# Two attention layers on one core: output projections of layer 0 grouped, two pairs' scores in a row at some block ends, normalisation in two parts

## The chip, the cores and the metric

The kernel runs on one core of one Trainium2 chip. A core has a matrix engine (TensorE, PE in the profile, with PEld for its weight loads), three engines for other arithmetic (VectorE or DVE, ScalarE or ACT, GpSimd or POOL), and a queue, SP, from which most transfers are issued. The metric is device time in microseconds (us). All data is 32-bit floating point.

## The reference

The input x has 4 batches of 128 channels and 64 x 64 = 4096 positions ("tokens"). Two layers follow one another.

Layer 0 is attention over all positions with a head of 64 channels, an output projection and a residual:

```
q, k, v = wq x, wk x, wv x            # 64 x 4096 each
att = softmax(k^T q)                  # 4096 x 4096
x   = x + wo (att applied to v)       # 128 x 4096
```

Layer 1 is causal attention over layer-normalised tokens with a head of 128, and then a recurrent FFN:

```
t = t + softmax(causal(LN(t) Wq (LN(t) Wk)^T / sqrt(128))) LN(t) Wv
h = LN(t) W, normalised over all 4 x 4096 tokens
y_t = sigmoid(h_t + V y_(t-1))        # along the tokens
t = t + y
```

## The kernel before, in words

The kernel has a fast path and a general path that is only entered where a check on the device fails; all that follows is the fast path.

**Tiles and loops.** The 4096 rows of an attention are done in 8 blocks of 512 (g = 0 to 7), the keys in tiles of 128. One step of the main loop deals with a pair of key tiles. In layer 0 every block has 16 pairs; in layer 1, which is causal, block g has 2g + 2. The order is: batch 0 layer 0 (128 pairs), batch 0 layer 1 (72 pairs), batch 1 layer 0, and so on. For a pair,

- `scores` makes a 128 x 1024 tile of scores in PSUM (s_ps, two buffers) and ScalarE takes the exponential into p (four buffers, tag "p" of pool "prob");
- `values`, two pairs later (SKEW = 2), multiplies p with the values and adds to the accumulator acc in PSUM, of which there is one buffer. Layer 0 works with the array split in tiles of 64 x 64 for scores and values, layer 1 and all projections with the full 128 x 128;
- `sums` adds p to dsum on VectorE, for the softmax's denominators. A p buffer is free when values and sums have both read it.

**The end of a block.** With the last pair's values, `values` empties the accumulator: in layer 0 ScalarE copies it to "half" (128 x 1024) and VectorE adds the two halves into agg. VectorE also adds the two halves of dsum into den. A chain of later steps is then started, `finish0` or `finish1`, a Python generator: each `yield n, step` asks for the step n pairs later. One due step at most is run per pair; where none is due, one of the list `side` is run, which holds the next batch's queries, keys and values.

In layer 0 the chain is: `folded` (sums of den over partitions, through a transpose on VectorE and DMAs to and from DRAM); then `project`, which is not run when due but put on a list `fill`, from which one entry is taken at the end of the next block of layer 0, or of a block g > 0 of layer 1; then `normed`, one pair later; then `by_channels`, two pairs after that, which turns the normalised tokens around through DRAM into xhT. So block g is projected at the end of block g + 1, and block 7 at the end of layer 1's block 1. `project` makes reciprocals of the denominators, four products of 128 columns into o_ps (one buffer of the two that all small PSUM uses share), and four operations on VectorE that join the result to the residual in xs. `normed` makes the layer norm on VectorE: statistics and their aggregation for four groups of tokens, the variance, a power of -1/2 on GpSimd (ln_rstd, line 458), one Newton step of four small operations on VectorE (lines 459 to 462), and four operations that write xh.

In layer 1 `finish1` does the same work with `wv1` for its projection, stores xs to x2, normalises, transposes, and multiplies with the FFN's weights (wx_ps). VectorE takes statistics of that product and ScalarE copies it into xs.

`rows1`, called at the end of the block two before, makes the rows of layer 1's block from xhT (r_ps). So layer 1's block 6 asks for xhT's block 6 at the end of its block 4.

**The order of the work.** The Python order of these calls is not the order on the engines: the framework reorders instructions within an engine, and `keep_in_program_order` pins an instruction to its place. [...] On TensorE the order around the change is: scores, values, scores, values, and at a block's end projection or rows, if any.

The lines named later: L806 and L815 scores of layers 0 and 1, L820 and L822 their exponentials, L866 and L874 values, L846 sums, L885 half, L605 products of the projection, L610 joins, L570 rows, L745 and L755 statistics and copy of the FFN product, L458 to L462 power and Newton step.

Of the kernel before, what the change touches and what calls it, by code (L numbers as in the profile page):

```python
# [9 lines left out]
F32 = mybir.dt.float32  # L10
AF = mybir.ActivationFunctionType
ALU = mybir.AluOpType
# [3 lines left out]
P = 128  # L16
BLK = 512
# [332 lines left out]
def fast_path(  # L350
# [105 lines left out]
    def rsqrt(y, var, z):  # L456

        nc.gpsimd.tensor_tensor(y, var, mhalf[:, : y.shape[-1]], ALU.pow)  # L458
        nc.vector.tensor_tensor(z, y, y, ALU.mult)  # L459
        nc.vector.tensor_tensor(z, z, var, ALU.mult)  # L460
        nc.vector.tensor_scalar(z, z, -0.5, 1.5, ALU.mult, ALU.add)
        nc.vector.tensor_tensor(y, y, z, ALU.mult)  # L462

    with tc.tile_pool(name="batch", bufs=1) as batch, tc.tile_pool(name="rows", bufs=2) as rowp, tc.tile_pool(
# [7 lines left out]
        def misc(name):  # L472
            return ps_m.tile([P, BLK], F32, tag="m", name=name)
# [23 lines left out]
        bs = [Batch() for _ in range(B)]  # L497
        for bt in bs:
            bt.next = []


        def cols0(b, m):
# [91 lines left out]
                nc.sync.dma_start(out=own, in_=by_token.rearrange("q r k j -> (q r) k j"))  # L594
            return own

        def project(layer, b, g, agg, own):

            rec = recs[:, layer, b, ts(g, TPB)]

            tc.keep_in_program_order(nc.vector.tensor_reduce(rec, own.rearrange("p q j -> p j q"), AX.X, ALU.add))
            nc.vector.reciprocal(rec, rec)
            op = misc("o_ps")
            for j in range(TPB):
                nc.tensor.matmul(  # L605
                    op[:, ts(j, P)], lhsT=agg[:, ts(j, P)], rhs=wv1 if layer else wo2, start=True, stop=True
                )
            for j in range(TPB):
                t = xs[:, b, ds(g * BLK + j * P, P)]
                nc.vector.scalar_tensor_tensor(  # L610
                    t, in0=op[:, ts(j, P)], scalar=rec[:, j : j + 1], in1=t, op0=ALU.mult, op1=ALU.add
                )

        def normed(b, g, dst):

            st = stat.tile([P, TPB, nc.vector.BN_STATS_DIM], F32, tag="st", name="ln_st")
            mv = stat.tile([P, TPB, nc.vector.BN_AGGR_DIM], F32, tag="mv", name="ln_mv")
            for j in range(TPB):
                nc.vector.bn_stats(st[:, j], xs[:, b, ds(g * BLK + j * P, P)])  # L619
                nc.vector.bn_aggr(mv[:, j], st[:, j])  # L620
            var = stat.tile([P, TPB], F32, tag="var", name="ln_var")
            nc.vector.tensor_scalar(var, mv[:, :, 1], LN_EPS, None, ALU.add)  # L622
            y = stat.tile([P, TPB], F32, tag="rstd", name="ln_rstd")
            rsqrt(y, var, stat.tile([P, TPB], F32, tag="z", name="ln_z"))
            for j in range(TPB):
                nc.vector.tensor_scalar(  # L626
                    dst[:, j], xs[:, b, ds(g * BLK + j * P, P)], mv[:, j, 0:1], y[:, j : j + 1], ALU.subtract, ALU.mult
                )
# [31 lines left out]
        def finish0(b, g):  # L660

            agg, den = bs[b].agg, bs[b].den

            def norm():
                if g == 0:
                    bs[b].xh = batch.tile([P, NT, P], F32, tag="xh", name="xh")
                    bs[b].xhT = batch.tile([P, N], F32, tag="xhT", name="xhT")
                normed(b, g, bs[b].xh[:, ts(g, TPB)])
# [13 lines left out]

            def rest():
                yield 1, norm
                yield 2, by_channels

            def first():
                own = folded(den, False)

                def second(s):  # L690
                    project(0, b, g, agg, own)
                    push(s, rest())

                fill.append(second)

            yield 1, first

        def finish1(b, g):
            agg, den = bs[b].agg, bs[b].den
# [9 lines left out]
            def first():  # L709
                if final:  # L710

                    nc.scalar.activation(spare, agg[:, 0:1], AF.Sigmoid)
                project(1, b, g, agg, mem["own"])
# [7 lines left out]
                normed(b, g, mem["xh"])  # L721

            def second():
                mem["xhT"] = wk.tile([P, BLK], F32, tag="xhT2", name="xhT2")
# [37 lines left out]
            def sums():  # L762
                mem["own"] = folded(den, by_pe)

            if by_pe:
                yield 1, lambda: (sums(), first())
            else:
                yield 1, sums
                yield 3, first
            yield 3, second  # L770
            yield 1 if final else 6 if g < 2 or g == NB - 1 else 4, third


# [82 lines left out]
        def values(it):  # L856

            bt = bs[it.b]
            if it.first:
                bt.acc = ps_a.tile([P, 2, BLK], F32, tag="a", name="acc")  # L860
            for h, (t, q0, n, o) in enumerate(it.at):
                if it.layer == 0:

                    for r in range(2):
                        part = slice(r * M, r * M + M)
                        nc.tensor.matmul(  # L866
                            bt.acc[h * M : h * M + M, r],
                            lhsT=bt.v[part, t % (NT // 2), t // (NT // 2)],
                            rhs=it.p[part, o : o + n],
                            start=it.first,  # L870
                            stop=it.last,
                        )
                else:
                    nc.tensor.matmul(  # L874
                        bt.acc[:, 0, q0:],
                        lhsT=bt.xh[:, t],
                        rhs=it.p[:, o : o + n],
                        start=it.first and h == 0,
                        stop=it.last and h == 1,
                    )  # L880
            if it.last:
                bt.agg = wk.tile([P, BLK], F32, tag="agg", name="agg")
                if it.layer == 0:
                    half = wk.tile([P, 2, BLK], F32, tag="half", name="half")
                    nc.scalar.copy(half, bt.acc)  # L885
                    nc.vector.tensor_tensor(bt.agg, half[:, 0], half[:, 1], ALU.add)
                else:
                    nc.scalar.copy(bt.agg, bt.acc[:, 0])
                bt.den = wk.tile([P, BLK], F32, tag="den", name="den")
                nc.vector.tensor_tensor(bt.den, it.den[:, 0], it.den[:, 1], ALU.add)  # L890

        waiting = []
        fill = []

        def push(slot, chain):
            step = next(chain, None)
            if step:
                waiting.append((slot + step[0], step[1], chain))
# [36 lines left out]
        started = []  # L935
        rows()
        rows()
        for s in range(len(items) + SKEW + 16):
            if s < len(items):
                it = items[s]  # L940
                if it.first:
                    bs[it.b].rows = bs[it.b].next.pop(0)
                    if it.layer and it.g == 3 and it.b + 1 < B:
                        for m in range(NB // 2):
                            side += keys(it.b + 1, m)
                scores(it)
            if 0 <= s - SKEW < len(items):
                it = items[s - SKEW]
                values(it)
                if it.last:  # L950
                    rows()
                    tokens()

                    if fill and (it.layer == 0 or it.g):
                        fill.pop(0)(s)
                    push(s, (finish1 if it.layer else finish0)(it.b, it.g))
            if s < len(items):
                sums(items[s])
# [12 lines left out]
        assert not waiting and not side and not fill  # L971

# [161 lines left out]
```

## Time and profile before

| | |
|---|---|
| median of 3 runs | 2074.14 us (2073.96 to 2077.06) |
| the profiled execution's own time | 2073.56 us |
| its span, first to last instruction | 2071.9 us |
| PE, PEld busy | 2052.6, 894.6 us |
| DVE, ACT, POOL busy | 1488.9, 993.6, 117.8 us |
| instructions of PE, DVE, ACT, POOL | 11716, 2865, 1071, 221 |
| clock granted to TensorE | 0.998 |

By stretches of the timeline, layer 0 of a batch takes some 237 us (242 in the first) and layer 1 some 257 us; the FFN's recurrence after the last block takes about 80 us.

How to read it: the page comes from one profiled execution. "busy" is the sum of an engine's instructions. Matmuls overlap and their ends are modelled, so two starts say more than one duration. In the timeline each row has start and duration in us, engine, source line, operation, output<-inputs, their shapes, and how many alike were merged; brackets hold the idle time before it and what ended that. A 32-bit product shows as two matmul instructions: 8 rows of s_ps or acc in layer 0 are the scores or values of one pair. "PE acc L866 <- ACT half L885" reads: that matmul waited for that copy.

### The profile page before, as it was taken

Reading aid. Unit: us, or ns where it says so; the run is one execution under the profiler, and the core shown is the slowest. Engines: PE = TensorE matmul, PEld = TensorE weight load, DVE = VectorE, ACT = ScalarE, POOL = GpSimd, SP = SyncE. Lnnn points to the kernel's source line nnn. Section 1 sums busy time; section 2 is a strip of 40 time slices with the busy share of each in tenths; the row PEclk is TensorE's granted clock in tenths of the full one; section 3 lists DMA queues with packets and bytes.
Section 4 is the critical chain, followed back from the end, with each engine's and each line's share of the span. In section 5 each row is a group of like instructions: output and inputs, shape, how many; then the busy total and the mean of one; then the engine's idle time right before and its main releaser. Section 6 shows DMA issues by size and latency. Waiting matters only on the chain.

```text
span 2071.9 us, 30792 instructions
## 1 busy us (share of the span) xinstructions
PE 2052.6 (99%) x11716; PEld 894.6 (43%) x11716; DVE 1488.9 (72%) x2865; ACT 993.6 (48%) x1071; POOL 117.8 (6%) x221
## 2 busy tenths in 40 slices
PE   9999999999999999999999999999999999999998
PEld 3333354444333344444333335444433334444456
DVE  4899975544889986554689997554578998655578
ACT  5666632333666643333466663323366665333365
POOL 1000010000000011000000001000000001100000
PEclk9999999999999999999999999999999999999999
DMA  3110123200110113311010012230001011201044
GB/s 113 53 20 15 22 57 76 68 16 16 57 22 13 22 32 72 78 37 24 16 53 16 19 22 57 68 75 16 16 17 17 17 22 27 51 21 26 16 168 164
DMA packets 207149, 89.03 MB, mean 43 GB/s; under 512 B 140961, under 2 KB 189601, under 8 KB 205969
## 3 DMA queue, kind: packets, MB, share of 16 engines
q1 hardware_dynamic: 205984, 86.42, 16.6%
q8 instruction: 94, 1.54, 0.3%
q14 instruction: 63, 0.51, 0.1%
q0 software_dynamic: 288, 0.39, 0.1%
q10 hardware_dynamic: 720, 0.16, 0.0%
HBM read 45.84 MB, written 36.89 MB: 40 GB/s over the span
## 4 chain that ended last, share of the span: by engine, by line
PE 82%; DVE 14%; issue 1%; ACT 1%; POOL 1%; DMA 0%; DVEq 0%; ACTq 0%; POOLq 0%
PE s_ps L815 22%; PE acc L874 22%; PE s_ps L806 14%; PE acc L866 14%; DVE dsum L846 9%; PE o_ps L605 2%; PE y_ps L1031 2%; PE r_ps L570 1%; PE wx_ps L742 1%; PE kr_ps L513 1%; ACT p L820 1%; PE v_ps L525 1%; DVE xr L1052 1%; POOL ln_rstd L458 1%; DVE xs L610 1%
## 5 line engine op out<-in xcount | busy, mean ns | idle before, releaser
L846 DVE TENSOR_TENSOR dsum<-dsum,p 128x1024 f32<-128x1024 f32 x676 | 825.2, 1221 | 394.9 <-ACT p L822 304.5
L820 ACT ACTIVATE p<-s_ps,nshift 128x1024 f32<-128x1024 f32 x512 | 571.2, 1116 | 324.3 <-PE s_ps L806 267.3
L822 ACT ACTIVATE p<-s_ps 128x1024 f32<-128x1024 f32 (+2 forms) x288 | 274.5, 953 | 605.1 <-PE s_ps L815 591.2
L866 PE MATMUL acc<-p,v 64*64 64x512 f32 x4096 | 532.2, 590 | 1.9 <-ACT half L885 1.9
L806 PE MATMUL s_ps<-swap,kr 64*64 64x512 f32 x2048 | 528.2, 592 | 2.0 <-ACT p L820 1.8
L806 PE MATMUL s_ps<-kr 64*64 64x512 f32 x2048 | 528.2, 592 | 0.3
L815 PE MATMUL s_ps<-rows,xhT 128*128 128x512 f32 (+3 forms) x1152 | 502.9, 559 | 0.0
L874 PE MATMUL acc<-p,xh 128*128 128x512 f32 (+3 forms) x1152 | 500.9, 557 | 0.0
L874 PEld LDWEIGHTS acc<-p,xh 128*128 128x128 f32 x1152 | 216.2, 190 | 244.3 <-issue 233.7
L815 PEld LDWEIGHTS s_ps<-rows,xhT 128*128 128x128 f32 x1152 | 214.1, 190 | 245.5 <-issue 209.3
L866 PEld LDWEIGHTS acc<-p,v 64*64 64x64 f32 x4096 | 155.1, 133 | 284.8 <-issue 270.4
L806 PEld LDWEIGHTS s_ps<-swap,kr 64*64 64x64 f32 x2048 | 138.4, 133 | 138.8 <-issue 123.7
L806 PEld LDWEIGHTS s_ps<-kr 64*64 64x64 f32 x2048 | 138.4, 133 | 138.0 <-issue 121.0
L458 POOL TENSOR_TENSOR ln_rstd<-ln_var,mhalf 128x4 f32<-128x4 f32 x64 | 68.8, 1075 | 1181.5 <-DVE ln_var L622 1181.5
L854 DVE TENSOR_TENSOR dsum<-dsum,p 128x256 f32<-128x256 f32 (+1 forms) x120 | 55.9, 498 | 53.4 <-POOL p L826 53.4
L610 DVE SCALAR_TENSOR_TENSOR xs<-o_ps,recs,xs 128x128 f32<-128x128 f32 x256 | 73.4, 343 | 3.7 <-PE o_ps L605 0.5
L626 DVE TENSOR_SCALAR xh<-xs,ln_mv,ln_rstd 128x128 f32<-128x128 f32 x256 | 71.4, 342 | 2.2
L826 POOL TENSOR_SCALAR_AFFINE_SELECT p<-p 128x128 f32<-128x128 f32 x128 | 38.2, 322 | 511.9 <-ACT p L822 506.2
L619 DVE BATCH_NORM_STATS2 ln_st<-xs 128x6 f32<-128x128 f32 x256 | 63.5, 269 | 0.0
L459 DVE TENSOR_TENSOR ln_z<-ln_rstd 128x4 f32<-128x4 f32 x64 | 10.4, 163 | 69.9 <-POOL ln_rstd L458 69.9
L755 ACT COPY xs<-wx_ps 128x512 f32<-128x512 f32 x31 | 18.1, 585 | 72.0 <-DVE stats L745 72.0
L844 DVE COPY dsum<-p 128x1024 f32<-128x1024 f32 x60 | 41.0, 684 | 11.7 <-ACT p L822 8.1
(138 smaller groups left out, 1023.4 us busy)
## 6 DMA issues: line engine op xcount, KB each, us to landing
xs<-in_xT SPq DMA_DIRECT2D x32, 256.0 KB, 3.0
by_r<-sqT SPq DMA_DIRECT2D x128, 64.0 KB, 2.2
xhT<-by_r SPq DMA_DIRECT2D x128, 64.0 KB, 2.0
x<-xs SPq DMA_DIRECT2D x32, 256.0 KB, 2.3
xr<-x SPq DMA_DIRECT2D x8, 1024.0 KB, 11.9
out_x<-xr SPq DMA_DIRECT2D x16, 512.0 KB, 3.5
by_c<-sqT SPq DMA_DIRECT2D x124, 64.0 KB, 1.8
xhT<-by_c SPq DMA_DIRECT2D x31, 256.0 KB, 2.7
```

The lines of the kernel that those rows point to most:

```text
L458: nc.gpsimd.tensor_tensor(y, var, mhalf[:, : y.shape[-1]], ALU.pow)
L610: nc.vector.scalar_tensor_tensor(t, in0=op[:, ts(j, P)], scalar=rec[:, j : j + 1], in1=t, op0=ALU.mult, op1=ALU.add)
L619: nc.vector.bn_stats(st[:, j], xs[:, b, ds(g * BLK + j * P, P)])
L626: nc.vector.tensor_scalar(dst[:, j], xs[:, b, ds(g * BLK + j * P, P)], mv[:, j, 0:1], y[:, j : j + 1], ALU.subtract, ALU.mult)
L806: nc.tensor.matmul(ps[c * M : c * M + M, off : off + n], lhsT=bs[it.b].kr[part, h, ds(t % (NT // 2) * P + c * M, M)], rhs=rows[h], start=True,
L815: nc.tensor.matmul(ps[:, off : off + n], lhsT=lhsT, rhs=rhs, start=True, stop=True)
L820: nc.scalar.activation(it.p[:, :off], ps[:, :off], AF.Exp, bias=nshift)
L822: nc.scalar.activation(it.p[:, :off], ps[:, :off], AF.Exp, scale=float(P) ** -0.5)
L846: nc.vector.tensor_tensor(flat, flat, it.p, ALU.add)
L854: nc.vector.tensor_tensor(den[:, h, q0:], den[:, h, q0:], it.p[:, o : o + n], ALU.add)
L866: nc.tensor.matmul(bt.acc[h * M : h * M + M, r], lhsT=bt.v[part, t % (NT // 2), t // (NT // 2)], rhs=it.p[part, o : o + n], start=it.first ...
L874: nc.tensor.matmul(bt.acc[:, 0, q0:], lhsT=bt.xh[:, t], rhs=it.p[:, o : o + n], start=it.first and h == 0, stop=it.last and h == 1,)
```

## The change

- Projections of layer 0 are made at set places, named in a table `visits`: blocks 0 and 1 at the end of block 2, blocks 2 and 3 at the end of block 4, block 4 at the end of 6, block 5 at the end of 7, and blocks 6 and 7 at the ends of layer 1's blocks 2 and 3. The list `fill` is gone. Until then the block's result waits in its own part of xhT, which is allocated at the end of block 0 and into which agg is now written.
- `project` is split into `denominators` (asked for 9 pairs after the fold), `projected` (the products, at the visit) and `joined` (one pair later, or nine for the second block of a visit).
- `normed` is split: `moments` has statistics, variance and the power on GpSimd and follows the join; the Newton step (`newton`) and the writing of xh come one pair later, with the Newton step's first instruction pinned to program order. In `finish1` likewise, but for the very last block, where both follow at once.
- At the ends of layer 0's blocks that have no visit (0, 1, 3 and 5) the scores of two pairs are made in a row, ahead of the next values; where the next pair's scores are due, they are already done.

```diff
+    def newton(y, var, z, pinned=False):
+        ins = nc.vector.tensor_tensor(z, y, y, ALU.mult)
+        if pinned:
+            tc.keep_in_program_order(ins)
...
-        def project(layer, b, g, agg, own):
+        def denominators(layer, b, g, own):
             rec = recs[:, layer, b, ts(g, TPB)]
             tc.keep_in_program_order(nc.vector.tensor_reduce(rec, own.rearrange("p q j -> p j q"), AX.X, ALU.add))
             nc.vector.reciprocal(rec, rec)
+
+        def projected(layer, agg):
             op = misc("o_ps")
...
+            return op
+
+        def joined(layer, b, g, op):
...
-        def normed(b, g, dst):
+        def moments(b, g):
...
-            rsqrt(y, var, stat.tile([P, TPB], F32, tag="z", name="ln_z"))
+            nc.gpsimd.tensor_tensor(y, var, mhalf, ALU.pow)
+            return mv, var, y
+
+        def normed(b, g, dst, mv, var, y, pinned=True):
+            newton(y, var, stat.tile([P, TPB], F32, tag="z", name="ln_z"), pinned)
...
             def first():
                 own = folded(den, False)
-                def second(s):
-                    project(0, b, g, agg, own)
-                    push(s, rest())
-                fill.append(second)
+                mem.append(own)
+
+            def leave(late):
+                op = projected(0, agg)
+                def rest():
+                    yield 1 + late, lambda: (joined(0, b, g, op), mem.append(moments(b, g)))
+                    yield 1, norm
+                    yield 2, by_channels
+                return rest()
+
+            bs[b].leave[g] = leave
             yield 1, first
+            yield 9, lambda: denominators(0, b, g, mem[0])
...
             if by_pe:
-                yield 1, lambda: (sums(), first())
+                yield 1, lambda: (sums(), first(), final and norm())
             else:
                 yield 1, sums
                 yield 3, first
-            yield 3, second
+            if not final:
+                yield 1, norm
+            yield 2, second
...
             if it.last:
-                bt.agg = wk.tile([P, BLK], F32, tag="agg", name="agg")
                 if it.layer == 0:
+                    if it.g == 0:
+                        bt.xhT = batch.tile([P, N], F32, tag="xhT", name="xhT")
+                    bt.agg = bt.xhT[:, ts(it.g, BLK)]
...
-        fill = []
+        visits = [{2: (0, 1), 4: (2, 3), 6: (4,), 7: (5,)}, {2: (6,), 3: (7,)}]
...
+        done = -1
+        def begin(s):
+            nonlocal done
+            if done < s < len(items):
+                done = s
...
+                scores(it)
+
+        for s in range(len(items) + SKEW + 16):
+            begin(s)
+            if SKEW < s < len(items) - 1 and items[s - SKEW].first and items[s + 1].layer == 0:
+                ended = items[s - SKEW - 1]
+                if ended.layer == 0 and ended.g not in visits[0]:
+                    begin(s + 1)
...
-                    if fill and (it.layer == 0 or it.g):
-                        fill.pop(0)(s)
+                    for k, g in enumerate(visits[it.layer].get(it.g, ())):
+                        push(s, bs[it.b].leave[g](8 * k))
                     push(s, (finish1 if it.layer else finish0)(it.b, it.g))
```

More of the change, by code (lines that the diff above doesn't have):

```diff
@@ L458, in rsqrt @@
         nc.gpsimd.tensor_tensor(y, var, mhalf[:, : y.shape[-1]], ALU.pow)
-        nc.vector.tensor_tensor(z, y, y, ALU.mult)
+        newton(y, var, z)
+    def newton(y, var, z, pinned=False):
+        ins = nc.vector.tensor_tensor(z, y, y, ALU.mult)
+        if pinned:
+            tc.keep_in_program_order(ins)
         nc.vector.tensor_tensor(z, z, var, ALU.mult)
@@ L499, in fast_path @@
             bt.next = []
+            bt.leave = {}
         def cols0(b, m):
@@ L607, in project @@
                 )
+            return op
+        def joined(layer, b, g, op):
+            rec = recs[:, layer, b, ts(g, TPB)]
             for j in range(TPB):
@@ L662, in finish0 @@
             agg, den = bs[b].agg, bs[b].den
+            mem = []
             def norm():
@@ L666, in norm @@
                     bs[b].xh = batch.tile([P, NT, P], F32, tag="xh", name="xh")
-                    bs[b].xhT = batch.tile([P, N], F32, tag="xhT", name="xhT")
-                normed(b, g, bs[b].xh[:, ts(g, TPB)])
+                normed(b, g, bs[b].xh[:, ts(g, TPB)], *mem.pop())
             def by_channels():
@@ L681, in by_channels @@
                     )
-            def rest():
-                yield 1, norm
-                yield 2, by_channels
             def first():
                 own = folded(den, False)
-                def second(s):
-                    project(0, b, g, agg, own)
-                    push(s, rest())
-                fill.append(second)
+                mem.append(own)
[7 more added lines that the diff above has]
+            bs[b].leave[g] = leave
             yield 1, first
+            yield 9, lambda: denominators(0, b, g, mem[0])
         def finish1(b, g):
@@ L712, in first @@
                     nc.scalar.activation(spare, agg[:, 0:1], AF.Sigmoid)
-                project(1, b, g, agg, mem["own"])
+                denominators(1, b, g, mem["own"])
+                joined(1, b, g, projected(1, agg))
                 if final:
@@ L720, in first, with norm @@
                 mem["xh"] = wk.tile([P, TPB, P], F32, tag="xh2", name="xh2")
-                normed(b, g, mem["xh"])
+                mem["of"] = moments(b, g)
+            def norm():
+                normed(b, g, mem["xh"], *mem["of"], not final)
             def second():
@@ L887, in values @@
                 else:
+                    bt.agg = wk.tile([P, BLK], F32, tag="agg", name="agg")
                     nc.scalar.copy(bt.agg, bt.acc[:, 0])
@@ L892, in fast_path @@
         waiting = []
-        fill = []
+        visits = [{2: (0, 1), 4: (2, 3), 6: (4,), 7: (5,)}, {2: (6,), 3: (7,)}]
+        assert NB == 8
         def push(slot, chain):
@@ L937, in fast_path @@
         rows()
-        for s in range(len(items) + SKEW + 16):
-            if s < len(items):
+        done = -1
[3 more added lines that the diff above has]
+                done = s
                 it = items[s]
@@ L944, in fast_path @@
                         for m in range(NB // 2):
-                            side += keys(it.b + 1, m)
+                            side.extend(keys(it.b + 1, m))
                 scores(it)
+        for s in range(len(items) + SKEW + 16):
[4 more added lines that the diff above has]
+                    begin(s + 1)
             if 0 <= s - SKEW < len(items):
@@ L970, in fast_path @@
                     form_half()
-        assert not waiting and not side and not fill
+        assert not waiting and not side
     with tc.tile_pool(name="xr", bufs=1) as xrp, tc.tile_pool(name="y", bufs=2) as yp, tc.tile_pool(
```

## The prediction

> **What bounds the kernel now.** I read the page's busy times first, then its chain that ended last, then the waits by engine, then the timeline of TensorE (PE) at single places. The first two:
>
> ```profile
> PE 2052.6 (99%) x11716; PEld 894.6 (43%) x11716; DVE 1488.9 (72%) x2865; ACT 993.6 (48%) x1071; POOL 117.8 (6%) x221
> PE 82%; DVE 14%; issue 1%; ACT 1%; POOL 1%; DMA 0%; DVEq 0%; ACTq 0%; POOLq 0%
> ```
>
> PE is busy 99% and carries 82% of the chain, so time can come only out of the matrix stream. "Busy" hides small losses, because the ends of matmuls are modelled; they show in distances between starts. This is PE around the end of block 0 of batch 0, layer 0 (columns: start, duration):
>
> ```profile
> 51.01 0.59 PE L806 MATMUL s_ps<-swap,kr 64*64 64x512 f32 x2
> ...
> 51.87 1.04 PE L866 MATMUL acc<-p,v 64*64 64x512 f32 x8
> 52.73 0.60 PE L806 MATMUL s_ps<-swap,kr 64*64 64x512 f32 x2
> ...
> 54.19 0.64 PE L866 MATMUL acc<-p,v 64*64 64x512 f32 x1 [0.42 <-ACT half L885]
> ```
>
> A step (scores or values of one pair) takes 0.86 us from start to start (51.01, 51.87, 52.73). The last distance is 1.46: the next block's values need the only accumulator, which the copy "half" on ScalarE (ACT) still empties. **Loss 0.60**; in the other three batches 546.44 to 547.96, loss 0.66. The step after it is 0.05 long (0.91), as after every stop below.
>
> At the ends of blocks 1 to 5 an output projection stands in that place:
>
> ```profile
> 79.99 1.04 PE L866 MATMUL acc<-p,v 64*64 64x512 f32 x8
> 80.96 1.16 PE L605 MATMUL o_ps<-wo,agg 128*128 128x128 f32 x8
> 82.05 0.65 PE L806 MATMUL s_ps<-swap,kr 64*64 64x512 f32 x2
> ...
> 82.96 0.61 PE L866 MATMUL acc<-p,v 64*64 64x512 f32 x4
> ```
>
> Its four 128-column products are worth one step, 0.86. Distances are 0.97, 1.09, 0.91: **0.39 lost** per visit in going from 64*64 tiles to 128*128 and back.
>
> Third, VectorE (DVE). Sums of a block's first pairs run late behind projection and normalisation, where DVE also waits for GpSimd's (POOL's) power:
>
> ```profile
> 87.17 0.17 DVE L622 TENSOR_SCALAR ln_var<-ln_mv 128x4 f32<-128x4 f32 x1
> 88.58 0.16 DVE L459 TENSOR_TENSOR ln_z<-ln_rstd 128x4 f32<-128x4 f32 x1 [1.24 <-POOL ln_rstd L458]
> ```
>
> I call lag the time from the end of a pair's exponential to the start of its sum. It peaks at 5.13 at the visit of 80 us, then 5.42, 5.70, 5.85, 5.86, 4.96. A sum frees one of four p buffers, so large lag holds ACT, and then PE:
>
> ```profile
> 179.53 1.04 PE L866 MATMUL acc<-p,v 64*64 64x512 f32 x8
> 180.60 0.65 PE L806 MATMUL s_ps<-kr 64*64 64x512 f32 x2
> ```
>
> 1.07 for 0.86. The losses are 0, 0, 0.07, 0.22, 0.23, 0 for those six lags: above about 5.65 PE loses what the lag exceeds. With 0.05 after each, **0.67 per batch**.
>
> Fourth, a place in batches 1 to 3 where layer 1's last FFN product meets the lag:
>
> ```profile
> 543.01 0.59 ACT L755 COPY xs<-wx_ps 128x512 f32<-128x512 f32 x1 [3.27 <-DVE stats L745]
> ```
>
> The statistics start at 542.29 behind eight back-to-back sums, the ACT copy waits for them, exponentials queue behind the copy, and PE goes from 543.03 to 544.67: **0.84 lost** with the 0.05.
>
> [...]
>
> **The change, part by part.** In the order of the changed program, layer 0 has eight o_ps products in a row at the ends of blocks 2 and 4, four beside r_ps at the end of 6 and four at the end of 7 as before; blocks 6 and 7 follow in layer 1 at the ends of its blocks 2 and 3. Ends 0, 1, 3, 5 have scores, scores, values, values. The products themselves are as many as before: nothing there.
>
> 1. Visits at 1, 3, 5 go: 3 x 4 batches x 0.39 = **-4.7**. Their "half" must now be hidden by the second scores, as at block 0. At 52.73 the second would start at 53.59 (its buffer is free: that exponential ended at 53.23) and end at 54.45, after 54.19, when values could run; in batch 1, 548.16 after 547.96. Cover is 0.26 and 0.20 to spare. Without it each end would lose 0.71.
> 2. Block 0's stop goes: 0.65 + 3 x 0.71 = **-2.8**.
> 3. Second products in 8 visits: between nothing (same mode) and 0.11 (r_ps at 225.21, o_ps at 226.18: 0.97 for 0.86). I take 0.05: **+0.4**. One more projection per batch in layer 1, where 256.91, 257.80, 259.57 give 0.03 and 0.06: 4 x 0.09 = **+0.4**.
> 4. Lag. Normalisation is split, so a sum stands between variance and newton; DVE's 1.24 wait becomes useful. But the order puts both blocks' joins and moments right behind the double visit; only the second newton comes seven sums later. From 83.22 of the trace: join and statistics as before to 85.85; three of the second block's joins (0.26 each) and two short ones, 86.9. The third pair's exponential now ends about 85.2 (visit 0.9 longer): lag 1.7. Then sum 1.14, the last join and second statistics 1.6, two sums 2.5, newton 0.81, xh 1.16, transpose 0.64: 94.7 against the sixth exponential's end at 90.4: **lag 4.4**. Seven sums recover 0.39 each (1.72 pitch less 1.33), the second newton part adds 2.6: 4.2. Three more sums and den, fold and transpose at the block's end (+1.6, as 0.43 became 2.05 at 107) give about 4.7, on a short copy. All below 5.65; by the end of the block without visit it is worked off (12 x 0.39). So 4 x 0.67 = **-2.7**.
> 5. At 527.15 the variance is ready; the sum that began at 528.37 can go before the wait, so the chain up to 531.88 is 0.9 earlier, and so are the eight sums and the copy of 543.01. PE lost 0.79 there, so it fits: 3 x 0.84 = **-2.5**.
> 6. Layer 1: pinned newtons on DVE, with sums, statistics and the by-channel DMAs on SP behind them. A layer 1 pair holds PE 3.43 us against DVE's 1.33, and PE has no wait there: nothing. Without that cover a POOL wait is 1.2 for each of 40. Blocks 6 and 7 come about 70 us later, but their rows are asked for only at the ends of blocks 4 and 5 of layer 1, 30 us or more after the visit; two DMA hops at 2.2 and 2.0 us fit. The order of SP's queue keeps the denominators' DMAs ahead of their use by several pairs. The tail after the last block keeps its order: nothing.
>
> Sum: -4.7 - 2.8 + 0.8 - 2.7 - 2.5 = -11.9. The profiled execution took 2073.56 (span 2071.9 and 1.7 around it), so 2061.7; the median 2074.14 is 0.6 above it: **2062.3**.
>
> **Rivals.**
> - *Only the matrix part comes* (0.13): DVE's lag and the stop at 543 stay, because a burst of two blocks replaces the waits saved. Speaks for it: lag stood at 5.4 with one block. Against: my 4.4. 2062.3 + 5.2 = 2067.5.
> - *The cover fails* (0.06): "half" is scheduled behind one more exponential (1.12), and the 16 plain ends each lose 0.71. Gains 1 and 2 turn into 12 x (0.71 - 0.39) = +3.8 and 0: 2062.3 + 7.5 + 3.8 = 2073.6. Against: the new ACT order has "half" before both exponentials.
> - *Nothing is gained otherwise* (0.03): [...] near 2072.
> - *Slower* (0.04): the double burst at the ends of 2 and 4 overruns the p buffers. It decides when the eight bursts cost PE over 11.9, that is 1.5 each, lag 7.15 or 2.7 above my sum; at lag 7.5, 8 x 1.9 = 15: about 2077.
> - The main case holds 0.74.
>
> **How the numbers follow.** A change of 0.2% is 4.1 us, about what a measurement of this kernel can tell from none. Main case and first rival are beyond it: faster 0.87; cover and nothing: 0.09; slower 0.04. The main case has its own range 2059.5 to 2065: all of layer 0's extra distance is 7.0 per batch, of which 3.3 goes, and a different order of layer 1's v_ps excursions (0.36 each, twelve) may give or take 1.5. With the first rival to 2069, no more than 2 in 10 is outside.
>
> **What would show it.** Steps 1 and 2: PE waits on "half" near nothing; values at plain ends 0.86 after the second scores. Step 3: o_ps to o_ps 0.86 to 0.97. Step 4: no wait on POOL in layer 0, lag peaks under 5.65 and no 1.07 distances. Step 5: the copy after the statistics near 542 minus what came before, with PE at 0.86. Layer 1 near 257 us per batch, as now. Wrong would be: "half" or p waits on PE, lag above 5.65, or longer layer 1.

## The result, and the profile after

| | before | changed kernel |
|---|---|---|
| median (range, runs) | 2075.43 us (2073.96 to 2077.06, 6) | 2066.5 us (2064.51 to 2067.79, 6) |
| ratio | | 0.9956, interval 0.9943 to 0.9969 |
| profiled execution, its span | 2073.56, 2071.9 us | 2065.22, 2063.5 us |
| first scores start at | 12.90 | 13.90 |
| from there to the end of the span | 2059.0 us | 2049.6 us |

The change makes the kernel 0.44% faster, 8.9 us by the medians. The forecast was 2062.3 with a range of 2059.5 to 2069.0, so the sign and the range held, and the likeliest case was 4.2 us too fast. The main case's own range ended at 2065; the result is inside the stated range only because that was stretched to 2069 for the first rival. The six times before fall into two groups, 2073.96 to 2074.14 and 2076.72 to 2077.06, with the median between them, so the 8.9 is known to a microsecond or two only.

The fifth row is the one to compare kernels by. The start of a profile varies: the first scores wait for the first transfers, and they began between 12.9 and 15.0 in the profiles of this study; two profiles of the changed kernel itself have 13.90 and 13.30. From the first scores on, the change is worth 2059.0 - 2049.6 = **9.4 us**, where the sum of the prediction had 11.9. Most of this section asks where those 2.5 us went.

First the page of the changed kernel, busy times and chain:

```profile
PE 2046.0 (99%) x11716; PEld 896.4 (43%) x11716; DVE 1492.2 (72%) x2865; ACT 990.1 (48%) x1071; POOL 135.5 (7%) x221
PE 97%; DVE 1%; issue 1%; DMA 0%; ACT 0%; POOL 0%; DVEq 0%; POOLq 0%; ACTq 0%
```

The counts are the same as before, so nothing was saved in work. VectorE has gone from 14% of the chain to 1%. One number has grown that the change was not meant to touch: GpSimd's busy time, from 117.8 to 135.5.

Second, TensorE around the end of block 0 of batch 0, the place shown at 51.87 before:

```profile
52.88 1.04 PE L895 MATMUL acc<-p,v 64*64 64x512 f32 x8
53.73 0.60 PE L835 MATMUL s_ps<-swap,kr 64*64 64x512 f32 x2
...
54.59 0.60 PE L835 MATMUL s_ps<-swap,kr 64*64 64x512 f32 x2
...
55.45 1.90 PE L895 MATMUL acc<-p,v 64*64 64x512 f32 x16
```

and ScalarE there:

```profile
54.13 1.01 ACT L917 COPY half<-acc 128x1024 f32<-128x1024 f32 x1
```

Starts are 52.88, 53.73, 54.59, 55.45: three steps of 0.86. The copy "half" ends at 55.14 and the accumulator is needed at 55.45. Before, where the values did wait, they began 0.05 behind the end of the copy (at 54.19, for 54.14), so of the 0.31 some 0.26 is to spare; in the first blocks of the other batches it is 0.20. The stop of 0.60 is gone, and no matmul of TensorE waits on "half" any more. (Its weight loads, which run ahead, still show 16 such waits of at most 0.5; they delay no matmul.)

Third, the first double visit, at the end of block 2:

```profile
107.81 1.04 PE L895 MATMUL acc<-p,v 64*64 64x512 f32 x8
108.78 2.05 PE L614 MATMUL o_ps<-wo,xhT 128*128 128x128 f32 x16
110.76 0.65 PE L835 MATMUL s_ps<-swap,kr 64*64 64x512 f32 x2
...
111.67 1.04 PE L895 MATMUL acc<-p,v 64*64 64x512 f32 x8
```

From 107.81 to 111.67 are 3.86 us for four steps' worth of work, one of values, two of projections, one of scores; four steps of 0.86 are 3.44, which leaves 0.42. A single visit lost 0.39 before. The second product of a visit costs 0.03 beyond its own step.

Fourth, VectorE behind that visit, at the first normalisation:

```profile
117.19 0.17 DVE L636 TENSOR_SCALAR ln_var<-ln_mv 128x4 f32<-128x4 f32 x1
117.27 2.55 DVE L875 TENSOR_TENSOR dsum<-dsum,p 128x1024 f32<-128x1024 f32 x2
119.73 0.16 DVE L462 TENSOR_TENSOR ln_z<-ln_rstd 128x4 f32<-128x4 f32 x1
```

Two sums stand between variance and Newton step, and there is no idle time. Of the 64 Newton steps, all of which waited for the power before, five still do. The lag (end of an exponential to start of its sum) peaks at 4.13 behind this visit and at 4.27 at the end of block 3, and is back at 0.03 before block 4 ends, where the next visit is. Both are under 5.65, and no step of 1.07 is left.

Fifth, the place where the forecast failed, layer 1's last FFN product in batch 1. The power and the start of the Newton step there before, on GpSimd and VectorE:

```profile
527.25 1.01 POOL L458 TENSOR_TENSOR ln_rstd<-ln_var,mhalf 128x4 f32<-128x4 f32 x1 [16.70 <-DVE ln_var L622]
```

```profile
528.29 0.16 DVE L459 TENSOR_TENSOR ln_z<-ln_rstd 128x4 f32<-128x4 f32 x1 [1.13 <-POOL ln_rstd L458]
```

VectorE in the changed kernel:

```profile
525.68 0.17 DVE L636 TENSOR_SCALAR ln_var<-ln_mv 128x4 f32<-128x4 f32 x1
525.76 1.22 DVE L875 TENSOR_TENSOR dsum<-dsum,p 128x1024 f32<-128x1024 f32 x1
527.88 0.16 DVE L462 TENSOR_TENSOR ln_z<-ln_rstd 128x4 f32<-128x4 f32 x1 [0.90 <-POOL ln_rstd L638]
...
530.46 10.49 DVE L875 TENSOR_TENSOR dsum<-dsum,p 128x1024 f32<-128x1024 f32 x8
540.87 0.69 DVE L772 BATCH_NORM_STATS2 stats<-wx_ps 128x6 f32<-128x512 f32 x1
```

GpSimd, ScalarE and TensorE at the same place, one fence each:

```profile
525.93 1.91 POOL L638 TENSOR_TENSOR ln_rstd<-ln_var,mhalf 128x4 f32<-128x4 f32 x1 [16.69 <-DVE ln_var L636]
```

```profile
541.59 0.59 ACT L782 COPY xs<-wx_ps 128x512 f32<-128x512 f32 x1 [3.16 <-DVE stats L772]
```

```profile
541.72 1.04 PE L895 MATMUL acc<-p,v 64*64 64x512 f32 x8
...
543.25 0.65 PE L835 MATMUL s_ps<-swap,kr 64*64 64x512 f32 x2 [0.49 <-ACT p L849]
```

The sum does stand ahead of the Newton step now. But the step waits all the same, 0.90 where it was 1.13, because the power that took 1.01 before takes **1.91** here. The copy's wait shrinks only from 3.27 to 3.16, half of the 0.23 that the Newton step gained: before, a sum filled the gap between the Newton step's first two instructions, and now nothing does. ScalarE's next exponential starts 0.49 behind the start of the copy in both kernels (at 543.50 before, at 542.08 now), and TensorE still goes 1.53 in place of 0.86.

The stops of TensorE follow the copy's wait closely. It was 3.27 before with a stop of 0.79, and is 3.16 now with 0.67: in both cases the wait less 2.48 or 2.49. The remaining experiments give more points of this line.

### The profile page after: what moved, and what is told of

Same layout as the page of the kernel before. It is cut to its first block, busy times and chain, and to the rows that moved or that the text cites. A ratio compares the mean times of both kernels' runs of the same rounds, so it can differ in the third digit from the quotient of the medians.

```text
span 2063.5 us, 30798 instructions
## 1 busy us (share of the span) xinstructions
PE 2046.0 (99%) x11716; PEld 896.4 (43%) x11716; DVE 1492.2 (72%) x2865; ACT 990.1 (48%) x1071; POOL 135.5 (7%) x221
## 4 chain that ended last, share of the span: by engine, by line
PE 97%; DVE 1%; issue 1%; DMA 0%; ACT 0%; POOL 0%; DVEq 0%; POOLq 0%; ACTq 0%
PE s_ps L844 22%; PE acc L903 22%; PE s_ps L835 22%; PE acc L895 21%; PE o_ps L614 3%; PE y_ps L1077 2%; PE r_ps L577 1%; PE wx_ps L769 1%; PE kr_ps L520 1%; PE v_ps L532 1%; DVE xr L1098 1%; PE warm_ps L484 0%; DMA swap<-kr 0%; ACT p L849 0%; DMA out_x<-xr 0%
## 5 line engine op out<-in xcount | busy, mean ns | idle before, releaser
L638 POOL TENSOR_TENSOR ln_rstd<-ln_var,mhalf 128x4 f32<-128x4 f32 x64 | 89.4, 1397 | 1102.1 <-DVE ln_var L636 1102.1
L1079 DVE SCALAR_TENSOR_TENSOR z<-xs,scale,y_ps 128x256 f32<-128x256 f32 x104 | 46.8, 480 | 2.9 <-PE y_ps L1077 1.7
```

Of the source, the lines that this page charges most:

```text
L638: nc.gpsimd.tensor_tensor(y, var, mhalf, ALU.pow)
```

## Experiments

All are edits of the changed kernel. The times are medians; "from the first scores" is the span less the start of the first scores in the profiled execution. The first four ran on one chip (before: 2074.48 there), the next four on another (before: 2074.13). A ninth, which only measures GpSimd, was run once.

| kernel | median (range, runs) | ratio to before, interval | from the first scores | against the changed kernel |
|---|---|---|---|---|
| scores never in a row | 2075.66 (2074.94 to 2078.66, 12) | 1.0005, 0.9996 to 1.0013 | 2060.2 | +10.6 |
| one projection per end | 2068.85 (2068.12 to 2069.99, 7) | 0.9968, 0.9957 to 0.998 | 2053.5 | +3.9 |
| normalisation whole | 2078.48 (2077.44 to 2081.31, 20) | 1.0019, 1.0013 to 1.0026 | 2064.5 | +14.9 |
| Newton step one pair later | 2062.5 (2061.8 to 2065.29, 4) | 0.9942, 0.9925 to 0.9958 | 2047.0 | -2.6 |
| changed kernel again | 2066.31 (2064.52 to 2066.98, 5) | 0.9958, 0.9944 to 0.9972 | 2049.6 | 0.0 |
| last FFN product later | 2063.77 (2062.66 to 2066.02, 5) | 0.9947, 0.9933 to 0.9961 | 2050.8 | +1.2 |
| rows at layer changes | 2061.66 (2061.52 to 2062.09, 5) | 0.9937, 0.9923 to 0.995 | 2046.9 | -2.7 |
| Newton later and rows | 2059.29 (2058.84 to 2061.96, 5) | 0.9928, 0.9914 to 0.9941 | 2044.2 | -5.4 |

The changed kernel gave 2049.6 from the first scores in both of its profiles, so the last two columns can be read to a few tenths where the medians, with ranges of up to 4, cannot. Two profiles, of "normalisation whole" and of "last FFN product later", hold 1.7 and 2.6 that belong to TensorE's clock, as told below.

### Scores never in a row

```diff
-                if ended.layer == 0 and ended.g not in visits[0]:
+                if False:
```

> The changed kernel without the two pairs' scores in a row; all else as in the change. My theory (the second scores hide the copy of the accumulator at the ends of blocks 0, 1, 3 and 5): PE stops at these 16 ends again, 0.71 us each, +11.4, near 2078 us, and the values' wait on the copy named half returns at 16 places. Rival (the copy would be ready anyway once VectorE is less behind): no change, 2066.

TensorE, at the end of block 0:

```profile
53.95 0.60 PE L835 MATMUL s_ps<-swap,kr 64*64 64x512 f32 x2
...
55.41 1.09 PE L895 MATMUL acc<-p,v 64*64 64x512 f32 x8 [0.42 <-ACT half L917]
```

and its waits (waited for, total us, times, longest):

```profile
PE acc L895 <- ACT half L917: 6.9, 16, 0.5
```

The stop is back, 1.46 for 0.86, and at all 16 ends of layer 0 that have no projection, not at four as before the change. That costs 10.6, and the kernel is where it was before, 1.0005. It is there only because it keeps the split of the normalisation. By an estimate from these figures, grouping alone loses: twelve new stops of 0.60 and 0.05 after each are 7.8, and the grouped visits save some 4.0. An end without a projection shows the copy that the projection had covered. Grouping and the second scores earn their time together.

### One projection per block end

```diff
-        visits = [{2: (0, 1), 4: (2, 3), 6: (4,), 7: (5,)}, {2: (6,), 3: (7,)}]
+        visits = [{1: (0,), 2: (1,), 3: (2,), 4: (3,), 5: (4,), 6: (5,), 7: (6,)}, {2: (7,)}]
```

> The changed kernel with one projection at the end of each of layer 0's blocks 1 to 7 and the last in layer 1, normalisation still in two parts, two scores in a row at the end of block 0 alone. My theory (a visit costs 0.39 us of tile mode, the second product in a visit nearly nothing): +4.7 for 12 more visits, -0.7 for the fewer second products and layer 1 projections: 2070.5 us; lag of the sums under 5.65, no loss by it. Rival (grouping the visits is what keeps VectorE's lag down): another 2.7, 2073 us, with steps of 1.07 us again.

Measured +3.9, with the lag peaking at 2.81 and no wait for p on TensorE but the three at the FFN product. So the split removes the lag stops, with or without grouping; grouping is worth its saved excursions and no more. It even raises the lag, from 2.81 to 4.27, which is free as long as it stays under the threshold.

### Normalisation in one step

```diff
-                    yield 1 + late, lambda: (joined(0, b, g, op), mem.append(moments(b, g)))
-                    yield 1, norm
-                    yield 2, by_channels
+                    yield 1 + late, lambda: (joined(0, b, g, op), mem.append(moments(b, g)), norm())
+                    yield 3, by_channels
```

Likewise in `finish1`, and the Newton step is not pinned.

> The changed kernel with power, Newton step and writing of xh in one piece right behind the statistics, not pinned, as before the change; visits and scores as in the change. The order then has both blocks' normalisation in one burst behind a double visit. My theory (PE loses what the lag exceeds 5.65 us): lag near 8.7 us, 3 us lost at each of the 8 double visits, near 2089 us. Rival (VectorE is 72% busy and its lag is hidden): 2066 us, as the change. A third (the wait for the power, 1.2 us each, is all that the split saves): below 2070.

TensorE at the first double visit:

```profile
123.04 1.04 PE L892 MATMUL acc<-p,v 64*64 64x512 f32 x8
...
125.77 0.65 PE L832 MATMUL s_ps<-swap,kr 64*64 64x512 f32 x2 [1.70 <-ACT p L846]
```

Slower than the kernel before, 1.0019: the mechanism of the rival "slower" is real, and the split is what keeps it away. The threshold of 5.65, taken from three small losses before the change, carries far beyond them. At the first visit the lag peaks at 8.16 and TensorE loses 1.87 and then 0.60, 2.47 together; 8.16 - 5.65 = 2.51. At the second it peaks at 7.12 and the losses are 0.83 and 0.60: 1.43 against 1.47. The other six visits lose 1.42 to 1.45 each, some 12.5 in all. The slowdown was smaller than expected, for only the first of the eight visits has the large lag. The rest of the 14.9 is mostly 1.7 at the start of the FFN's recurrence, in this profile alone; it belongs to the clock (below).

### The Newton step of layer 1 one pair later

The power's 1.91 had a suspect. In the changed kernel it takes 1.01 in 35 of 64 cases, in each of which no sum on VectorE had started before it or the sum started at least 0.08 later. It takes 1.91 to 2.14 in 25 cases, in each of which a sum was running, or started within 0.02. In four more it takes 1.43, beside an addition of 0.69. So the suspect is the sum that runs beside the power.

If so, one sum cannot cover a power that is issued behind it, for the power is done only 0.87 after the sum. Two sums can. The transpose is still asked for at the same pair as in the changed kernel.

```diff
             if not final:
-                yield 1, norm
-            yield 2, second
+                yield 2, norm
+            yield 2 if final else 1, second
```

> The changed kernel with layer 1's Newton step two pairs behind the statistics instead of one, and the transpose one pair later, so that two sums stand between variance and Newton step. My theory of the stop near 541 us that the change left [...]: the wait of 0.9 us goes, statistics and copy come 0.9 earlier against PE, the stop of 0.68 to 0.80 us goes in three batches: -2.3, near 2064 us. Rival (the statistics stand behind eight sums, whatever the power does): the stop stays, 2066 us.

VectorE at the place of 525 above:

```profile
524.81 0.17 DVE L636 TENSOR_SCALAR ln_var<-ln_mv 128x4 f32<-128x4 f32 x1
524.89 2.55 DVE L875 TENSOR_TENSOR dsum<-dsum,p 128x1024 f32<-128x1024 f32 x2
527.35 0.15 DVE L462 TENSOR_TENSOR ln_z<-ln_rstd 128x4 f32<-128x4 f32 x1
...
529.93 9.16 DVE L875 TENSOR_TENSOR dsum<-dsum,p 128x1024 f32<-128x1024 f32 x7
539.00 0.69 DVE L772 BATCH_NORM_STATS2 stats<-wx_ps 128x6 f32<-128x512 f32 x1
```

and GpSimd and ScalarE:

```profile
525.06 1.91 POOL L638 TENSOR_TENSOR ln_rstd<-ln_var,mhalf 128x4 f32<-128x4 f32 x1 [16.70 <-DVE ln_var L636]
```

```profile
539.73 0.58 ACT L782 COPY xs<-wx_ps 128x512 f32<-128x512 f32 x1 [2.17 <-DVE stats L772]
```

The power is as slow as in the changed kernel, 1.91, but now two sums cover it, and the 0.90 is gone. As many sums stand ahead of the statistics, 2 + 7 for 1 + 8. The copy waits 2.17 in place of 3.16, which is 0.99 less, and all three stops are gone; 2.17 is below 2.49. The kernel gains 2.6, of which the three stops of 0.67 to 0.80 and the step of 0.05 after each are 2.3. So it is the wait on the held-up power that kept step 5's stop alive; the rival, that the eight sums behind it are enough, falls.

### GpSimd beside the sums

To measure the suspect itself, GpSimd was given work that nothing uses, timed by the exponential that it reads from.

```diff
+    probe = const.tile([P, 2 * P], F32, name="probe")
...
                     nc.vector.tensor_tensor(flat, flat, it.p, ALU.add)
+                    if it.layer == 0 and it.g == 1:
+                        nc.gpsimd.tensor_tensor(probe[:, :TPB], it.p[:, :TPB], mhalf, ALU.pow)
+                        nc.gpsimd.memset(probe, 0.0)
+                    if it.layer == 0 and it.g == 3:
+                        nc.gpsimd.tensor_copy(probe, it.p[:, : 2 * P])
+                        nc.gpsimd.memset(probe, 0.0)
```

> The changed kernel with work on GpSimd added that nothing uses: in layer 0, behind each sum of block 1, a power that reads p (128x4, as in the normalisation) and a memset (128x256); behind each sum of block 3 a copy that reads p (128x256) and the same memset. Theory [...]: powers and copies issued while a sum runs take until the sum's end and then their own time; the memset, which reads nothing, takes the same time beside a sum and beside none. [...] Rival (GpSimd is late for another reason, its own dispatch or the semaphore): the power's times do not follow the sums, and the memset is long beside sums too.

GpSimd and then VectorE in block 1 of batch 0:

```profile
71.66 1.27 POOL L878 TENSOR_TENSOR probe<-p,mhalf 128x4 f32<-128x4 f32 x1
```

```profile
70.83 1.23 DVE L876 TENSOR_TENSOR dsum<-dsum,p 128x1024 f32<-128x1024 f32 x1 [0.49 <-ACT p L850]
```

The sum runs to 72.06, the power starts at 71.66: 0.40 of the sum is left, and the power takes 1.27 = 0.40 + 0.87. GpSimd in batch 1, and a copy in block 3:

```profile
552.84 2.06 POOL L878 TENSOR_TENSOR probe<-p,mhalf 128x4 f32<-128x4 f32 x1
554.96 0.31 POOL L879 MEMSET probe<- 128x256 f32 x1
555.36 1.01 POOL L878 TENSOR_TENSOR probe<-p,mhalf 128x4 f32<-128x4 f32 x1
```

```profile
127.21 0.90 POOL L881 COPY probe<-p 128x256 f32<-128x256 f32 x1
```

The first power fell 0.03 behind a sum's start and takes 2.06 = 1.20 + 0.86; the second met a sum with 0.01 to run and takes 1.01. Spans on GpSimd are rough in a profile, but the starts say the same: the memset behind the first power starts 2.12 after it, and the one behind the second, at 556.42, 1.06 after it. Over all, 45 powers were issued beside a running sum. 39 of them take what is left of it and 0.86 to 0.87; the other six met 0.10 or less and take 1.01. All 36 such copies take what is left and 0.25 to 0.26, where a copy that met nothing on VectorE takes 0.40. The memset takes 0.30 to 0.31 beside all 83 sums that it met. So the powers and copies on GpSimd waited for the end of the sum beside them, and the memsets did not.

Sums are not the only ones that hold GpSimd up: VectorE's copy dsum<-p (L874) and its writing of xh (L646) did so too. Beside dsum<-p a copy took 0.74 with 0.49 left, and even the memset 0.77 or 0.78, three times; beside xh a copy took 0.47 with 0.22 left. There VectorE was slowed as well: the four instructions of xh took 1.30 together beside copies and memsets, and 1.12 in the changed kernel.

The sums were not held up in turn. They take 1.18 to 1.24 whether a power was ahead of them or not: a power at 59.00 took 1.01 with a sum from 59.09 that took 1.23. Nor do they start late: behind a power from 60.46 the sum starts at 60.49, 0.03 after its exponential ended, as sums do elsewhere. A tiny power ahead of a sum cost neither of them anything here; the same power just behind it cost 0.9. A large read by GpSimd ahead of a sum was not tried.

The added work cost the kernel nothing that shows (2049.5 from the first scores).

### The last FFN product later

```diff
-            yield 1 if final else 6 if g < 2 or g == NB - 1 else 4, third
+            yield 1 if final else 12 if g == NB - 1 else 6 if g < 2 else 4, third
```

> The product with the FFN's weights of layer 1's last block is asked for 12 pairs after the transpose instead of 6; the split normalisation with its wait for the power (0.90) stays. Theory (the stop is a meeting: the statistics of that product stand behind the late sums, the copy behind the statistics, exponentials behind the copy): after six more pairs VectorE has worked the lag off, so all three stops of 0.68 to 0.80 go though the wait for the power is still there: 2.0 to 2.3 us below the changed kernel. Rival (the late sums hold PE by themselves, whatever the product does): the stops stay or move with it, 0 to 0.5 us.

ScalarE in batch 1:

```profile
550.94 0.59 ACT L782 COPY xs<-wx_ps 128x512 f32<-128x512 f32 x1 [2.71 <-DVE stats L772]
```

The stops become 0.22, 0.22 and 0.35, a gain of 1.4, not 2.0 to 2.3. The lag was not worked off: six pairs later the product meets the end of a block, with the addition of the halves of dsum, its transpose and the join of "half" on VectorE, and a new row of sums. Both theory and rival were too simple, but the three stops fall on the line: waits of 2.71 and, in batch 3, 2.84, stops of 0.22 and 0.35, each the wait less 2.49.

By the profile this kernel is 1.2 slower than the changed one, by the medians 2.5 faster. Windows of the profile at the start of the recurrence explain it (stretch, its length, then busy time and count of PE, PEld, DVE, ACT and POOL, the granted clock, DMA share, GB/s), first for this kernel:

```profile
1984.00:1988.00 4.00, 4.00 (x10) 3.19 (x10) 1.27 (x8) 2.07 (x4) 0.03 (x1) 0.50 0.95 395
```

and for the changed kernel again:

```profile
1984.00:1988.00 4.00, 3.45 (x15) 2.75 (x16) 1.43 (x9) 1.79 (x4) 0.55 (x1) 1.00 0.89 328
```

In that execution the clock fell to 0.50 behind the pauses of the last normalisation, and matmuls that start 0.22 apart in the changed kernel start 0.43 apart. From the last values to the recurrence it took 16.62, and 14.03 in the changed kernel: 2.6 longer. The profile of "normalisation whole" shows the same, with a mean of 0.74 over one stretch of 4 us, and took 15.71, 1.7 longer. In the other nine profiles the clock stays at 1.00 there. Why it fell in these two executions and not in the others, no run here shows.

### Two pairs' scores in a row where the layer changes

```diff
             begin(s)
+            if 0 < s < len(items) and items[s].layer != items[s - 1].layer:
+                begin(s + 1)
```

> Two pairs' scores in a row also where the layer changes (seven changes), so that the array's tiling changes once there and not three times. Theory (each change of tiling costs about half of an excursion of 0.39): two fewer at each of seven places, 2 x 0.18 x 7 = 2.5 us below the changed kernel. Rival (the first and last values of a block are held by the exponentials of the scores made early, so PE loses there what the tiling saves): 0 to 1 us, with p or acc waits on PE at the changes.

TensorE from layer 0 to layer 1 in batch 0, first in the changed kernel again:

```profile
247.50 1.04 PE L895 MATMUL acc<-p,v 64*64 64x512 f32 x8
248.47 1.77 PE L844 MATMUL s_ps<-rows,xhT 128*128 128x512 f32 x4
250.17 1.09 PE L895 MATMUL acc<-p,v 64*64 64x512 f32 x8
251.19 0.92 PE L844 MATMUL s_ps<-rows,xhT 128*128 128x256 f32 x4
252.04 1.09 PE L895 MATMUL acc<-p,v 64*64 64x512 f32 x8
253.06 1.12 PE L577 MATMUL r_ps<-xhT,g 128*128 128x512 f32 x2
```

then with the edit:

```profile
247.69 1.04 PE L895 MATMUL acc<-p,v 64*64 64x512 f32 x8
248.66 2.42 PE L844 MATMUL s_ps<-rows,xhT 128*128 128x512 f32 x8
251.01 1.95 PE L895 MATMUL acc<-p,v 64*64 64x512 f32 x16
252.89 1.12 PE L577 MATMUL r_ps<-xhT,g 128*128 128x512 f32 x2
```

The same work takes 5.20 in place of 5.56, for the tiling changes three times between these rows and no longer five. Over seven changes of layer the gain is 2.7, with 2.5 expected. No wait comes in its place.

### Both together

The edits are those of "Newton step one pair later" and of the rows.

> Both: the Newton step of layer 1 one pair later (two sums cover the held-up power) and two pairs' scores in a row where the layer changes. Theory: the two gains are in different places and add, 2.2 for the three stops and 2.5 for the tiling, 4.7 us below the changed kernel. Rival (one of the two delays the other, for the late Newton step falls behind the pairs made early): no more than the better of the two alone, 2.5 us or less.

The gains add: 5.4, with 2.6 and 2.7 for each alone, and by medians 7.0 against the changed kernel on the same chip. At 0.9928 of the kernel before (0.9914 to 0.9941) this version beats both.

## Why the prediction was right or wrong, step by step

From one layer's first scores to the next's, layer 0 is shorter by 3.29, 3.33, 3.34 and 3.21 in the four batches, and layer 1 longer by 0.98 in the first three. Each layer 0 has given one projection of 0.86 to its layer 1. Without it layer 0 gained 9.7, where steps 1 to 5 without layer 1's part had 12.3, and each of the three layers 1 lost 0.12.

- **Step 1, fewer visits, and step 2, block 0's stop: right.** No matmul waits on "half". The cover has 0.26 to spare in the first batch and 0.20 at the first block of the others, as predicted. That this cover is worth what it was priced at is shown by taking it away: +10.6.
- **Step 3, second products: right.** 0.03 against 0.05; the projection moved to layer 1 costs 0.12 against 0.09.
- **Step 4, lag: right in kind, 0.4 too large.** 1.53 and 4.13 where 1.7 and 4.4 were worked out, 4.27 for 4.7, and no loss. The threshold was confirmed to 0.04 at lags of 7.12 and 8.16. But "4 x 0.67" took the lags of batch 0 for all four. In batches 1 to 3 the third of the peaks was 5.57 and not 5.70, below the threshold, and PE lost 0.54 per batch there; in all that is 2.3 and not 2.7. The powers behind the visits are held up by a sum as well (1.92 at 117.44); the two sums that stand there cover that too, which the prediction did not know.
- **Step 5, the stop at the last FFN product: wrong, and nearly all of the gap.** The claim was that "the sum that began at 528.37 can go before the wait", so that the chain would be 0.9 earlier. That took the power's 1.01 from the kernel before, where VectorE stood idle beside it in the case looked at, and let it run beside a sum. Behind a sum's start it took 1.91, that is the sum's rest and some 0.87, so of the wait of 1.13 there remained 0.90, and the stops went from 0.79 each to 0.67, 0.67 and 0.80: 0.2 gained of 2.5. The kernel before showed it: its 64 powers took 1075 ns on average, more than the 1.01 of most, and one of them already had a sum ahead of its Newton step, as the change means to have it:

```profile
1949.22 1.22 DVE L846 TENSOR_TENSOR dsum<-dsum,p 128x1024 f32<-128x1024 f32 x1
```

```profile
1949.40 1.91 POOL L458 TENSOR_TENSOR ln_rstd<-ln_var,mhalf 128x4 f32<-128x4 f32 x1 [23.96 <-DVE ln_var L622]
```

```profile
1951.34 0.17 DVE L459 TENSOR_TENSOR ln_z<-ln_rstd 128x4 f32<-128x4 f32 x1 [0.90 <-POOL ln_rstd L458]
```

The 1.91 and the remaining wait of 0.90 were there to be read.

- **Step 6, layer 1 and the tail: right**, but for the 0.12 of step 3. The pinned Newton steps cost nothing there. A "longer layer 1" was a badly chosen sign of being wrong: by the prediction's own step 3 layer 1 takes over a projection, and it is 0.98 longer for that.

With the sizes measured the steps come to 4.7 + 2.8 - 0.3 - 0.4 + 2.3 + 0.2 = 9.3, and the profiles have 9.4. The rest of the 4.2 between forecast and median lies outside the sum: the profile's first scores came 1.0 later than before, and the median stands 1.3 above the profiled execution, not 0.6 as the forecast took from the three times before that it had.

Of the rivals, "only the matrix part comes" would have given 2067.5, near the 2066.5 measured, but for the wrong reason: of the two losses that it lets stay, those by lag went and only the stop at 543 stayed. That a time fits a rival does not make it true. "Slower" and "the cover fails" are real mechanisms, each shown by removing what stops it. "Nothing is gained otherwise", by which a visit saved would be paid for at the second product or in layer 1 all the same, falls with the 0.03 of a second product and the 0.12 in layer 1.

**What stays open.** The changed kernel's third stop (0.80) is 0.13 longer than the other two. It lies on the line of 2.49, for the copy waits 3.29 there. The 0.13 arises on VectorE: in batch 3 the second of the four joins starts 0.39 behind the first (at 1506.35) and 0.26 in batch 2 (at 1014.94). The trace names no wait there, and the cause is not known.

## What to carry to other kernels

Before an engine's wait is filled with other work, ask whether that work holds up the very thing waited for: the power priced here at 1.01 beside an idle VectorE took 1.91 beside a sum, and two sums of cover were needed where one had seemed enough. When work is grouped to save an overhead, look at what its old places were hiding; here grouping would have lost more than it saved, had nothing else covered the copy. Where a stop is the tail of a queue, find the slack of that queue first (in layer 0, 2.49 for the copy and 5.65 for the sums): here delays below it cost nothing, and those above it were paid in full.

## What was not expected of the hardware

- A GpSimd power of 128x4 took 1.01 alone or ahead of a VectorE sum, and the rest of the sum and 0.86 behind its start, up to 2.08 in the run with the added work. A GpSimd copy of 128x256 took 0.40, or the rest and 0.26. A memset took 0.31 beside sums and beside nothing, but 0.77 beside VectorE's copy dsum<-p. The sums stayed at 1.18 to 1.24 throughout; four instructions that write xh grew from 1.12 to 1.30 beside GpSimd's copies and memsets.
- A second group of 128*128 products inside one visit cost 0.03 beyond its own work, where the visit itself cost 0.39.
- Behind three pauses of TensorE (1.02, 0.35 and 1.41 us) within some 6 us, its granted clock fell (means of 0.50 and 0.74 over 4 us) in two of eleven profiled executions and not in the others, at a cost of 2.6 and 1.7 us.
